# Two attention blocks on one core: query and key projections by seven half products in place of eight, with the combinations formed on chip

## The chip, the cores and the metric

The kernel runs on one core of a Trainium2 chip. The metric is the device time of one execution in microseconds (us), the median of several runs.

## What is computed

Two layers, one after the other, on x of shape (4, 32, 32, 768): four images of 1024 tokens with 768 channels. Each layer is a group normalisation, an attention with 12 heads of 64 channels and a positional bias, an output projection and a residual. All is float32. Cut to what matters (layer 1 differs by biases on queries, keys and values, and by the scale):

```python
xn = gn(x)                                   # 32 groups of channels
qkv = xn @ Wqkv                              # 768 -> 3 * 768
q, k, v = split(qkv)                         # per head: 1024 x 64
rel_h = einsum('bhwc,hkc->bhwk', q, Rh)      # bias by row distance
rel_w = einsum('bhwc,wkc->bhwk', q, Rw)      # bias by column distance
scores = scale * q @ k.T + rel_h[..., :, None] + rel_w[..., None, :]
out = softmax(scores) @ v
x = x + out @ Wproj + bproj
```

## The kernel before

**Tiling.** Channels lie on the 128 partitions, six chunks of them (NC = 6), tokens along the free dimension. Eight images are worked on in turn (two layers of four), each in six pairs of heads: 48 pairs, numbered g. A pair has eight units n, one for each 128 query tokens.

**A unit** (the loop over `units`, L566) works on three units at once: `biases` (L312) adds the two bias parts into tiles sc of unit n+2 on POOL; `scores` (L326) multiplies queries by keys for unit n+1 into PSUM (two buffers of 128x1024, one a head), VectorE adds the bias and takes the extreme of each row (L342), and ACT takes the exponential with its row sum (L346); `turn` (L358) transposes the finished sc of unit n in blocks on VectorE into tb, and every second unit writes tb to DRAM (td, L373); `divide` (L351) takes the reciprocal of the sums of unit n+1 on VectorE (L353) and multiplies on POOL (L356). `read_back` (L378) fetches td in another order as pt, a quarter of the queries at a time, and `weigh` (L386) multiplies pt by the values: quarters 0 and 1 of the pair at n=6, quarters 2 and 3 at n=2 of the next pair.

**What fills TensorE between.** While pair g is worked on, `prepare(g + 1)` supplies the projections of the next pair. `project_in` (L202) has four groups (queries or keys, left or right half of the tokens), each of six chunk steps; a step is two products of 64 contracted rows, the upper and the lower half of the partitions, which go to two PSUM areas t[0] and t[1] (the two halves of the array work side by side). ACT copies t[0] to SBUF and VectorE adds t[1] (L227 to L230). `project_values` (L237) does the same for two pairs at once in four groups, two of them in each pair. `put_out` gives groups of the output projection. `take` (L524) hands these out step by step, in the numbers of `shares`: [6, 6, 0, 6, 12, 6, 0, 12] steps in units 0 to 7, 48 a pair.

**Order.** The order of instructions on each engine is the order in which this program writes them; no scheduler moves them. Almost all DMAs are issued by SP, in that order, and a DMA that waits holds up those behind it. Work appended to `later` is issued two units on, work appended to `early` one unit on. `positions` (L269) multiplies the queries by the table of distances and writes the result to DRAM; `diagonals` (L295) reads it back with sixteen DMAs as rel. They follow the query groups: positions two units after each, the diagonals at n=4. Read-backs of quarters 1 and 3 are issued in the unit after their td; those of 0 and 2 two units after.

**Input.** The normalised image lies in six tiles xn of 128x1024, from nine buffers (AHEAD = 3); `load_x` (L88) fills them, `stats` (L147) takes the means and variances of chunks, `norm` (L156) forms those of the groups, and `apply` (L192) normalises on VectorE, for the next image in pair 4. Weights: two buffers of one kind for queries and keys, one for values.

## Time and profile before

| | before |
|---|---|
| median of 3 runs, us | 3506.68 (3505.36 to 3508.88) |
| profiled execution, us | 3508.77 |
| its span, us | 3507.0 |
| granted TensorE clock | 0.998 |
| DMA moved | 1084.54 MB, 309 GB/s in the mean |

The span is the time from the first to the last instruction of the profiled execution; 1.8 us of that execution lie around it. The page gives for each engine its busy time and share, then the costliest groups of instructions: line, engine, operation, output<-input, shape, count, then busy time, mean nanoseconds of one, idle time in front, and what ended that idle time. Matmuls on the two halves of the array overlap, so the mean of one (591 ns for pj) is longer than what each adds to the time; the distance between the starts of two groups tells that. A float32 matmul of the program is two records in the profile.

### The profile page before, as it was taken

The numbers are of one execution on the slowest core, as the hardware profiler recorded it, in microseconds if no ns is written. First come the engines' busy times: TensorE is split into PE (matmuls) and PEld (weight loads), VectorE is DVE, ScalarE is ACT, GpSimd is POOL, SyncE is SP. The second block draws the span as 40 slices with busy tenths as digits, with TensorE's granted clock in tenths as the row PEclk, the third lists the DMA queues.
The fourth block names the chain that finished last, engine by engine and source line by source line (L and its number), as shares of the span: only waits on it lengthen the run. The fifth ranks groups of instructions, "written<-read, shape, count | busy, mean of one in ns | idle before, by whom it ended". The sixth has DMA issues, their size and how long they took to land.

```text
span 3507.0 us, 55102 instructions
## 1 busy us (share of the span) xinstructions
PE 3462.3 (99%) x21120; PEld 1921.4 (55%) x21120; DVE 2381.1 (68%) x3676; ACT 1227.5 (35%) x2040; POOL 2729.9 (78%) x1546
## 2 busy tenths in 40 slices
PE   6999999999999999999999999999999999999999
PEld 4555555555555555555555555555555555555554
DVE  4666767767677676767767667666666667666666
ACT  2334333333333333333333333333333333333331
POOL 3888887778777787788777788787787778787774
PEclk9999999999999999999999999999999999999999
DMA  4889989999899898898989989899889988898877
GB/s 137 312 308 311 332 293 337 319 316 326 304 329 323 313 316 313 312 324 305 326 305 326 320 292 332 311 331 306 300 327 324 321 298 316 319 322 295 311 275 281
DMA packets 624857, 1084.54 MB, mean 309 GB/s; under 512 B 247120, under 2 KB 310096, under 8 KB 575440
## 3 DMA queue, kind: packets, MB, share of 16 engines
q1 hardware_dynamic: 569008, 1028.29, 83.4%
q10 hardware_dynamic: 55584, 52.72, 4.4%
q8 instruction: 166, 2.72, 0.3%
q14 instruction: 99, 0.81, 0.1%
HBM read 580.59 MB, written 500.27 MB: 308 GB/s over the span
## 4 chain that ended last, share of the span: by engine, by line
PE 97%; DMA 2%; DVE 0%; SPq 0%; issue 0%; ACT 0%; POOL 0%; ACTq 0%; DVEq 0%
PE pj L214 28%; PE s L333 19%; PE av L399 19%; PE o L475 14%; PE pv L249 14%; PE tp L281 3%; DMA tdr<-t 1%; DMA pt<-td 1%; SPq L307 0%; DMA td<-tb 0%; DMA wo<-in_wo 0%; DMA xn<-in_x 0%; DVE st L152 0%; DMA rel<-tdr 0%; DMA per<-mv 0%
## 5 line engine op out<-in xcount | busy, mean ns | idle before, releaser
L319 POOL TENSOR_TENSOR sc<-rel 128x1024 f32<-128x1024 f32 x768 | 1890.4, 2485 | 38.2 <-DMA rel<-tdr 38.2
L356 POOL TENSOR_SCALAR sc<-sc,sm 128x1024 f32<-128x1024 f32 x768 | 855.1, 1127 | 686.1 <-DVE sm L353 669.2
L346 ACT ACTIVATE sc<-sc,sm 128x1024 f32<-128x1024 f32 x768 | 879.8, 1147 | 1370.9 <-DVE sm L342 1368.7
L342 DVE CUSTOM_DVE_ANT_0 sc<-s,sc 128x1024 f32<-128x1024 f32 x768 | 909.8, 1222 | 293.3 <-PE s L333 266.4
L214 PE MATMUL pj<-xn,w 64*128 64x512 f32 x4608 | 1033.5, 591 | 26.8 <-DVE xn L193 25.7
L370 DVE STREAM_TRANSPOSE tb<-sc 128x1024 f32<-128x1024 f32 x768 | 910.7, 1222 | 22.9 <-DMA td<-tb 20.5
L214 PEld LDWEIGHTS pj<-xn,w 64*128 64x128 f32 x4608 | 453.2, 188 | 568.6 <-issue 536.6
L333 PE MATMUL s<-k,q 64*128 64x512 f32 x3072 | 750.1, 598 | 7.0 <-DVE sm L342 6.9
L399 PE MATMUL av<-pt,v 128*64 128x256 f32 x6144 | 689.1, 382 | 6.1 <-DMA pt<-td 6.1
L399 PEld LDWEIGHTS av<-pt,v 128*64 128x64 f32 x6144 | 434.5, 137 | 289.8 <-ACT v L259 35.6
L249 PE MATMUL pv<-wv,xn 64*128 64x256 f32 x4608 | 515.7, 376 | 0.0
L249 PEld LDWEIGHTS pv<-wv,xn 64*128 64x128 f32 x4608 | 448.3, 187 | 90.8 <-issue 30.1
L475 PE MATMUL o<-attn,wo 128*128 128x512 f32 x1080 | 475.8, 597 | 0.2 <-DMA wo<-in_wo 0.2
L333 PEld LDWEIGHTS s<-k,q 64*128 64x128 f32 x3072 | 288.5, 187 | 299.5 <-issue 275.5
L475 PEld LDWEIGHTS o<-attn,wo 128*128 128x128 f32 x1080 | 201.4, 190 | 271.4 <-issue 260.9
L260 DVE TENSOR_TENSOR v<-pv,v 128x256 f32<-128x256 f32 x192 | 81.5, 425 | 277.6 <-ACT v L259 277.6
L259 ACT COPY v<-pv 128x256 f32<-128x256 f32 x192 | 71.5, 372 | 330.7 <-PE pv L249 282.9
L286 ACT COPY t<-tp 128x1024 f32<-128x1024 f32 x96 | 97.2, 1012 | 245.5 <-PE tp L281 148.5
L346 ACT ACTIVATION_READ_ACCUMULATOR sc<-sc,sm 128x1 f32 x768 | 143.6, 187 | 0.0
L230 DVE TENSOR_TENSOR q<-pj,q 128x512 f32<-128x512 f32 x96 | 66.4, 692 | 107.5 <-ACT q L227 56.0
L230 DVE TENSOR_TENSOR k<-pj,k 128x512 f32<-128x512 f32 x96 | 66.4, 692 | 95.5 <-ACT k L227 49.0
L281 PEld LDWEIGHTS tp<-tab,q 64*128 64x128 f32 x1536 | 100.0, 187 | 39.9 <-issue 39.6
(34 smaller groups left out, 787.6 us busy)
## 6 DMA issues: line engine op xcount, KB each, us to landing
td<-tb SPq DMA_DIRECT2D x384, 1024.0 KB, 5.9
pt<-td SPq DMA_DIRECT2D x382, 1024.0 KB, 7.6
tdr<-t ACTq DMA_DIRECT2D x96, 512.0 KB, 6.3
w<-in_wqk SPq DMA_DIRECT2D x96, 384.0 KB, 7.5
rel<-tdr SPq DMA_DIRECT2D x760, 32.0 KB, 2.3
part<-res SPq DMA_DIRECT2D x84, 256.0 KB, 5.5
res<-part SPq DMA_DIRECT2D x84, 256.0 KB, 9.1
wv<-in_wv SPq DMA_DIRECT2D x24, 768.0 KB, 8.7
```

The costliest lines, as they stand in the source:

```text
L214: nc.tensor.matmul(t[:, a, :], lhsT=w[rows, c, :], rhs=xn[c][rows, cols], start=(c == 0), stop=(c == NC - 1),)
L230: nc.vector.tensor_tensor(to, t[1], to, ALU.add)
L249: nc.tensor.matmul(t[:, a, k, :], lhsT=xn[c][rows, (2 * i + k) * P : (2 * i + k + 1) * P], rhs=w[rows, c, :], start=(c == 0), stop=(c == N ...
L281: nc.tensor.matmul(ps[:, h, j, :], lhsT=q[rows, at * P : (at + 1) * P], rhs=tabs[l][rows, :], start=True, stop=True,)
L319: nc.gpsimd.tensor_tensor(sc.rearrange("p (a k) (u l) -> p a (k u) l", a=4, l=8), rel[:, h, 0, n, :].unsqueeze(1).unsqueeze(3).to_broadcas ...
L333: nc.tensor.matmul(ps[h][:, cols], lhsT=q[rows, n * P : (n + 1) * P], rhs=k[rows, cols], start=True, stop=True,)
L342: nc.vector.tensor_tensor_reduce(out=sc, in0=ps[h], in1=sc, scale=-scale, scalar=BIG, op0=ALU.add, op1=ALU.min, accum_out=st[:, 0, h : h + 1],
L346: nc.scalar.activation(sc, sc, AF.Exp, bias=st[:, 0, h : h + 1], scale=-1.0, accum_out=st[:, 1, h : h + 1],)
L356: nc.gpsimd.tensor_scalar(sc, sc, st[:, 2, h : h + 1], 1.0, ALU.mult, ALU.mult)
L370: nc.vector.transpose(tb[:, :, j, :], sc_of[g, n, h])
L399: nc.tensor.matmul(av[rows, at * 2 * P : (at + 1) * 2 * P], lhsT=v_of[g][:, k, rows], rhs=pt_of[g, quarter, h][:, :, k, :], start=(k == 0) ...
L475: nc.tensor.matmul(t, lhsT=wo_of[im, o, c], rhs=attn_of[im * NP + c][:, cols], start=(c == c0), stop=(c == c1 - 1),)
```

## The change

A product of two matrices cut into two by two blocks needs seven block products in Strassen's scheme instead of eight, at the price of sums of blocks. Here the blocks are the upper and lower half of the 128 partitions of a chunk (TOP and LOW) on the contracted side, queries and keys on the one outer side and the two halves of the tokens on the other. It is used for 39 of the 48 pairs; pair 0 of each image, and pair 1 of the first, stay `plain`.

- `project_in` has four units. Units 0, 2 and 3 have six chunk steps as before, each step two half products; unit 1 has three, since its one half product is spread over both halves of the partitions. `shares` gives 9 steps in n=0 and 6 in n=4 for these pairs (45 in all).
- `sum_weights` forms the weights' sums once for each of the 39 pairs, one pair ahead of the projection, at n=6 (ACT) and n=7 (VectorE and POOL). `sum_input` forms the input's sums once an image during pair 5 of the image before (for the first image during its pair 0), one chunk in each of n=0 to 5, and at n=6 and 7 subtracts the left from the right half in place.
- The right half's values are then restored in `project_values`: the products of the left half's upper rows are kept in v where the right half will come (`part`), and are added.
- x is in 21 tiles of 128x512, handed on from image to image by `make_room`. For the statistics of layer 0 all chunks pass through the tmp buffer; the loads for use come in pair 4. `apply` is on POOL for all images but the first.
- The transposed tile tb has two buffers instead of three. The weights w0, w1, w3 and w4 have one each. The table of layer 1 is loaded late into the place of that of layer 0. The last image's outputs lie in tiles of x.
- `biases` runs over the same elements in another order: the innermost loop has 32 elements with a step of 8 in the output.

```diff
-    tbpool = ctx.enter_context(tc.tile_pool(name="tb", bufs=3))
+    tbpool = ctx.enter_context(tc.tile_pool(name="tb", bufs=2))
...
+    def make_room(im):
+        x, y = x_of[im - 1], y_of[im - 1]
+        x_of[im] = y[NC:] + x[:NC] + y[:3]
+        y_of[im] = y[3:NC] + x[NC:]
...
-        def apply(c):
-            nc.vector.tensor_scalar(
-                xn_of[im][c], xn_of[im][c], nrm[:, c, 0:1], nrm[:, c, 1:2], ALU.subtract, ALU.mult
+        def apply(c, i):
+            x = x_of[im][i * NC + c]
+            (nc.gpsimd if im else nc.vector).tensor_scalar(
+                x, x, nrm[:, c, 0:1], nrm[:, c, 1:2], ALU.subtract, ALU.mult
             )
...
+            w, x = (
+                (w_of[g, 0], xs[:NC]), (w_of[g, 4], ys[NC:]),
+                (w_of[g, 3], xs[NC:]), (w_of[g, 1], ys[:NC]),
+            )[unit]
...
+        elif unit == 0:
+            nc.scalar.copy(k[0], t[0])
+            add(q[0], t[1], k[0], bias[0])
+        elif unit == 1:
+            add(k[0], t[0], k[0])
+            add(k[0], t[1], k[0])
+        elif unit == 2:
+            add(k[1], t[0], k[0])
+            add(q[1], t[1], k[1], bias[0])
         else:
+            add(k[1], t[0], k[1], bias[1])
+            add(k[0], t[0], k[0], bias[1])
+            nc.vector.tensor_tensor(k[0], k[0], t[1], ALU.subtract)
...
+        if g + 1 < NPAIR:
+            if unit == (1 if plain(g) else 0):
+                later.append(lambda: load_w(g + 1, 0))
+            if unit == 3:
+                early.append(lambda: load_w(g + 1, 1))
...
+        def first():
+            nc.scalar.copy(w3[TOP], w[1][LOW])
+
+        def second():
+            nc.vector.tensor_tensor(w3[TOP], w3[TOP], w[1][TOP], ALU.add)
+            nc.gpsimd.tensor_tensor(w3[LOW], w3[TOP], w[0][TOP], ALU.subtract)
+            nc.vector.tensor_tensor(w4[TOP], w3[TOP, :3], w[0][TOP, :3], ALU.subtract)
+            nc.vector.tensor_tensor(w4[LOW], w3[TOP, 3:], w[0][TOP, 3:], ALU.subtract)
+            nc.gpsimd.tensor_tensor(w3[LOW], w[0][LOW], w3[LOW], ALU.subtract)
+            nc.gpsimd.tensor_tensor(w[1][TOP], w[0][TOP], w[1][TOP], ALU.subtract)
...
+    def sum_input(im, n):
+
+        xs, ys = x_of[im], y_of[im]
+        if n < NC:
+            a, b, y, z = xs[n], xs[NC + n], ys[n], ys[NC + n % 3]
+            nc.scalar.copy(y[LOW], b[TOP])
+            nc.vector.tensor_tensor(y[TOP], b[LOW], y[LOW], ALU.subtract)
+            if n < 3:
+                nc.vector.tensor_tensor(z[TOP], y[TOP], a[TOP], ALU.add)
+                nc.vector.tensor_tensor(y[LOW], y[TOP], a[TOP], ALU.add)
+                nc.vector.tensor_tensor(y[LOW], y[LOW], a[LOW], ALU.subtract)
+            else:
+                nc.vector.tensor_tensor(z[LOW], y[TOP], a[TOP], ALU.add)
+                nc.vector.tensor_tensor(y[LOW], z[LOW], a[LOW], ALU.subtract)
+            return
+        for c in range(3 * (n - NC), 3 * (n - NC) + 3):
+            a, b = xs[c], xs[NC + c]
+            (nc.gpsimd if c < 3 else nc.vector).tensor_tensor(b[TOP], b[TOP], a[TOP], ALU.subtract)
...
-            nc.scalar.copy(to, t[:, 0, :, cols])
-            nc.vector.tensor_tensor(to, t[:, 1, :, cols], to, ALU.add)
+            part = v_of[g + h][:, 2 * i + 4 : 2 * i + 6, :] if i < 2 and g else to
+            if i < 2 or g == 0:
+                nc.scalar.copy(part, t[:, 0, :, cols])
+            else:
+                nc.vector.tensor_tensor(to, t[:, 0, :, cols], to, ALU.add)
+            nc.vector.tensor_tensor(to, t[:, 1, :, cols], part, ALU.add)
...
-            shape = [P, 4, HW, 8]
+            shape = [P, 4, 8, HW]
             nc.gpsimd.tensor_tensor(
-                sc.rearrange("p (a k) (u l) -> p a (k u) l", a=4, l=8),
-                rel[:, h, 0, n, :].unsqueeze(1).unsqueeze(3).to_broadcast(shape),
-                rel[:, h, 1, n, :].rearrange("p (l a) -> p a l", a=4).unsqueeze(2).to_broadcast(shape),
+                sc.rearrange("p (a k) (u l) -> p a l (k u)", a=4, l=8),
+                rel[:, h, 0, n, :].unsqueeze(1).unsqueeze(2).to_broadcast(shape),
+                rel[:, h, 1, n, :].rearrange("p (l a) -> p a l", a=4).unsqueeze(3).to_broadcast(shape),
...
-                shares = [6, 6, 0, 6, 12, 6, 0, 12]
+                shares = [6, 6, 0, 6, 12, 6, 0, 12] if g + 1 >= NPAIR or plain(g + 1) else [9, 6, 0, 6, 6, 6, 0, 12]
...
+            if pair == 4 and not end:
+                if n == 0:
+                    make_room(im + 1)
+                for c in range(3 * n - 3, 3 * n) if 1 <= n <= 4 else ():
+                    load_x(im + 1, c % NC, c // NC)
...
-            if pair == 4 and n == 7 and not end:
-                for chunks in ((3, 4), (5,)):
-                    take(todo, 3)
-                    share -= 3
-                    for c in chunks:
-                        apply(c)
+            if pair == 4 and n in (6, 7) and not end:
+                for c in range(4) if n == 6 else range(4, NX):
+                    apply(c % NC, c // NC)
+            if g + 2 < NPAIR and not plain(g + 2) and n in (6, 7):
+                if n == 6:
+                    sums = sum_weights(g + 2)
+                sums[n - 6]()
+            if pair == NP - 1 and not end:
+                sum_input(im + 1, n)
+            elif g == 0:
+                sum_input(0, n)
```

## The prediction

> **What bounds the kernel now.** I read the page from the top: busy time by engine, the slices, the chain of waits; then the cost groups, the list of waits, and stretches of the timeline around one pair of heads.
>
> ```profile
> PE 3462.3 (99%) x21120; PEld 1921.4 (55%) x21120; DVE 2381.1 (68%) x3676; ACT 1227.5 (35%) x2040; POOL 2729.9 (78%) x1546
> ...
> PE 97%; DMA 2%; DVE 0%; SPq 0%; issue 0%; ACT 0%; POOL 0%; ACTq 0%; DVEq 0%
> PE pj L214 28%; PE s L333 19%; PE av L399 19%; PE o L475 14%; PE pv L249 14%; PE tp L281 3%; DMA tdr<-t 1%; DMA pt<-td 1%; SPq L307 0%; DMA td<-tb 0%; DMA wo<-in_wo 0%; DMA xn<-in_x 0%; DVE st L152 0%; DMA rel<-tdr 0%; DMA per<-mv 0%
> ...
> L319 POOL TENSOR_TENSOR sc<-rel 128x1024 f32<-128x1024 f32 x768 | 1890.4, 2485 | 38.2 <-DMA rel<-tdr 38.2
> L356 POOL TENSOR_SCALAR sc<-sc,sm 128x1024 f32<-128x1024 f32 x768 | 855.1, 1127 | 686.1 <-DVE sm L353 669.2
> ```
>
> TensorE is 97% of the chain, and pj, the group that the change cuts, is its largest part. POOL has 686 us of idle in front of the divides; that is the whole margin it has. VectorE is at 68%. So TensorE work taken away is time taken away, unless something that now hides beneath it comes out. Where that could be, the timeline shows (start, length, engine, line, shape, count):
>
> ```profile
> 1722.03 1.89 PE L333 MATMUL s<-k,q 64*128 64x512 f32 x8
> 1723.75 5.32 PE L214 MATMUL pj<-xn,w 64*128 64x512 f32 x24
> 1728.90 1.88 PE L333 MATMUL s<-k,q 64*128 64x512 f32 x8
> 1730.61 5.32 PE L214 MATMUL pj<-xn,w 64*128 64x512 f32 x24
> 1735.76 5.35 PE L249 MATMUL pv<-wv,xn 64*128 64x256 f32 x48
> 1740.94 1.88 PE L333 MATMUL s<-k,q 64*128 64x512 f32 x8
> ```
>
> ```profile
> 1727.62 1.46 SPq L373 DMA_DIRECT2D td<-tb  x2
> 1729.17 10.31 SPq L307 DMA_DIRECT2D rel<-tdr  x16
> 1739.59 0.94 SPq L381 DMA_DIRECT2D pt<-td  x2
> ```
>
> The first shows one unit n=3 (6.87 us) and one n=4 (12.04 us, two groups in it). The second shows SP's queue in the same time: the sixteen rel transfers take 10.3 us to issue, and the read-back of quarter 1 comes behind them.
>
> **What the skill says, and whether the trace agrees.** (1) The Trainium skill, "SBUF — State Buffer", section "Who interferes with whom": a VectorE instruction in a two-port mode, or with two SBUF inputs, contends with a GpSimd instruction that reads SBUF; whoever comes second is blocked for a whole instruction. The normalisation shows this for the two-port kind:
>
> ```profile
> L193 DVE TENSOR_SCALAR xn<-xn,nrm x48: 808/1204/2620, 24.9 to 2987.3; 128x1024 f32<-128x1024 f32 x48
> ```
> (min/median/max ns). Alone it takes 808 ns. Its mean is 1470 (69.6 us for 48); leaving out the first six, the mean is (69.6 − 6×0.81)/42 = 1.54, so the other engine costs 0.7 us each time. No VectorE operation of the kernel before has two SBUF inputs, so for these no row exists. (2) "GPSIMD Engine Reference", section "Performance pitfalls for Q7 kernels": a read with a step above 8 bytes costs about 2.9 cycles an element instead of 1.9; section "Performance versus the Vector engine": an add of 2048 elements takes 4497 ns. The bias add now reads one input with a step of 16 bytes; its 2.485 us for 1024 elements are 2.9 cycles at the page's 1.2 GHz, which agrees.
>
> **The change part by part**, against the profiled run of 3508.8 us (span 3507.0; the median of the runs is 3506.7, 2 us less).
>
> *Products removed.* 39 of 48 pairs aren't plain. In each, three of 24 chunk steps go, that is 12 matmul records of 512 columns (each step has four: two row halves, two passes). A group of 24 records and the start of the next are 1728.90 − 1723.75 = 5.15 us apart, 0.2146 each. 39 × 12 × 0.2146 = 100.4 us, all on the chain.
>
> *Combining products.* A plain pair drains four products by four ACT and four VectorE instructions (0.69 us each); the others by one and eight. Four more VectorE adds are 2.8 us a pair. Values 2 and 3 move their first copy to VectorE: 4 × 0.42 = 1.7 us in every second pair. One input of each is PSUM, so the contention above does not apply. Beneath TensorE: a unit of VectorE is 4.7 us from its first score reduction to the reciprocal, and units last 6.9 to 12.4.
>
> *Weights.* 39 times on VectorE three adds at n=7 (64x768, twice 64x384: about 0.9 + 0.5 + 0.5 us at the element rate of the 512-column row), plus blocking; on POOL three of 64x768, about 1.7 us each by the page's 4497/2048 ns an element, 5.1 us a pair. n=7 lasts 12.4 us, while POOL needs 7.1 for biases and divides: 12.2, just covered. The normalisation moves to POOL too, 84 of about 0.6 us, mostly in n=7 of pair 4.
>
> *Sums of the input.* Once an image, in pair 5 (for the first image in its pair 0), VectorE gets four 64x512 adds in n=0 to 2, three in n=3 to 5 and in n=7. They have two SBUF inputs, follow one another, and start just as POOL starts divides and biases. I take 0.62 us each and 0.6 us of blocking (from 0.0 to 1.1: the latter if each of them lets one POOL instruction pass). A unit is then 4.7 + 4×1.22 + 0.7 = 10.3 us for n=0 to 2, 9.1 for n=3, 9.9 for n=4, 9.2 for n=5, 5.4 for n=6 and 15.1 for n=7 (sums, weights, four outputs of 0.75); TensorE's units in these lines are 7.0, 7.8, 9.9, 6.9, 12.0, 6.9, 8.9, 12.4. VectorE falls behind by 3.3, 2.5, 0.4, 2.2, gains 2.1, loses 2.3, gains 3.5, loses 2.7. It may lag by about the unit less 3.4 us before the next scores find no free PSUM. Stepping through that, TensorE stands 2.7 us at n=3, 0.4 later, 1.1 at the next pair's start: 4.2 us an image, 34 us for eight. With 0 us of blocking nothing stands; with 1.1 us it is 9.6 an image, 77.
>
> *Read-back of quarter 1.* In the pairs with seven products n=4 takes 6 steps instead of 12: the weighing of n=6 comes 5.1 us earlier. The read-back doesn't: SP issues sixteen rel transfers first (10.3 us), and now also the second weight, which was behind it. Before, it was issued at 1739.6 and 1740.1, lands 7.6 us later (the page's median), 1747.7, and was needed half-way through the weighing at 1749.65 + 3.56 = 1753.2. Now it is needed at 1748.1 and lands at about 1748.2. Nothing is left over; with a scatter of one or two us I take 0.6 us a pair, 39 × 0.6 = 23 us (0 to 1.5 a pair).
>
> *Two buffers for the transposed tile instead of three.* The even units' transposes must wait for the write of the unit before. At 3 to 4 and 5 to 6 the gap is some 5.6 us, the median landing 5.9: VectorE waits about a microsecond, sometimes more, three times a pair. Beneath TensorE, as VectorE has about 58 of 70 us to do; uncovered it would be some 2 us a pair.
>
> *Bias add with the other loop order.* Reads become contiguous, writes get a step of 32 bytes. By the page's add, 2.25 us (estimate); nothing shows strided writes on POOL. Bounds 2.0 to 3.5. It is off the chain up to a point given below. The table of layer 1 loaded late, x in halves, 4.7 MB more of loads for statistics, other buffers for the last outputs: 0 (±3), as TensorE waits for none of them in the list of waits.
>
> Sum: 3508.8 − 100.4 + 34 + 23 = 3465; on the median's basis 3463.
>
> **Rivals.** *Everything stays hidden.* For it: engines other than TensorE have slack over any whole pair; two applications at n=2 and n=4 took 0.86 us, nearly unblocked. Against: they met POOL at a lucky moment. 3506.7 − 100.4 = 3406, to 3416. *The sums meet POOL one for one.* For it: the three applications of n=7 took 5.0 us instead of 2.4. 3463 + (77 − 34) = 3506, no change. *POOL becomes the bound (slower).* Place: the bias add, 768 times. Price: 77 us per 0.1 us. The rest of POOL is 855 + 199 (weights) + 50 (normalisation) + 26 (sums of n=6) = 1130 us, so POOL fills the 3406 us from 2.96 us an add and exceeds the old time from 3.1; at 3.3 it gives 3665. For it: if writes cost by their step as the page says of reads, 32 bytes is past its 8. Against: the old order had a read of that kind, which goes.
>
> **How the numbers follow.** Forecast 0.42, own range 3435 to 3495; all hidden 0.22; one for one 0.17 (it spills to both sides of no change); POOL bound 0.16; others 0.03. Under 0.2%, 7 us, a measurement of this kernel can't tell from no change. Faster: 0.42 + 0.22 + 0.06 + 0.01 = 0.71; same 0.06; slower 0.16 + 0.06 + 0.01 = 0.23. The range reaches from all hidden to just beyond one for one: 3405 to 3520, leaving out the bound by POOL.
>
> **What would show it.** 468 fewer pj records, of the same 0.21 us. In the list of waits, scores waiting for VectorE in each pair 5 and at n=3 above all, about 4 us an image; av waiting for pt by some 0.6 us a pair; the input's adds at about 1.2 us in the mean, with a minimum near 0.6; the bias add below 2.485 us. Wrong I am if the bias add is above 2.9, or if TensorE stands in ordinary pairs for something else: late weights, a drained product, the transposed tile's write.

## The result, and the profile after

| | before | after |
|---|---|---|
| median of 4 runs, us | 3507.62 (3505.36 to 3508.88) | 4081.73 (4075.33 to 4093.54) |
| ratio, 95% interval | | 1.1641 (1.1612 to 1.1671) |
| profiled execution, us | 3508.77 | 4075.33 |
| its span, us | 3507.0 | 4073.3 |
| granted TensorE clock | 0.998 | 0.947 |

The changed kernel is 16% slower, where the prediction had 3463 us and a range up to 3520. First the page of after: busy time by engine, the granted clock by slice, the chain of waits by engine and by line.

```profile
PE 3568.1 (88%) x20652; PEld 1936.1 (48%) x20652; DVE 2951.5 (72%) x4197; ACT 1177.7 (29%) x1918; POOL 2893.8 (71%) x1771
...
PEclk9999899998999989999899998999989999899999
...
PE 51%; DVE 19%; DMA 16%; POOL 7%; issue 4%; SPq 2%; ACT 0%; DVEq 0%; ACTq 0%
PE pj L262 17%; DMA td<-tb 12%; PE av L514 11%; PE s L448 10%; PE o L590 6%; PE pv L364 5%; DVE tb L485 5%; POOL x L223 4%; DVE sc L457 3%; DMA pt<-td 2%; PE tp L396 2%; SPq L422 2%; DVE x L334 2%; POOL sc L434 1%; DVE x L345 1%
```

TensorE has 468 records less than before (21120 to 20652), as the scheme promises, but the chain that ends last no longer runs through it: its share fell from 97% to 51%, and the write of the transposed tile (td<-tb) alone has 12%. Two amounts make up the 566 us. TensorE idles 505 us instead of 45 (span less busy time): 460 more. And it is busy 106 us longer in spite of 100 us less work: 3568.1 against 3462.3 − 100.4 = 3361.9, 206 us more. Most of that is the lower clock: the trace's clock records put TensorE at half clock for 434 us (17 before), it was busy in 292 of them, and half of those, some 146 us, would have been saved at full clock. The other 60 us are not explained. The list of waits says who is late (total, times, longest, in us); before, the first of these lines was 20.5 in all, 6.5 at most, and the second 6.1 in all:

```profile
DVE tb L485 <- DMA td<-tb: 378.0, 121, 9.6
PE av L514 <- DMA pt<-td: 110.6, 49, 4.1
PE o L590 <- DVE res L599: 103.0, 15, 15.5
PEld pj L262 <- POOL x L223: 88.7, 52, 3.4
PE o L590 <- DVE res L601: 84.0, 25, 4.6
```

So VectorE waits for the write (td, before its transposes), TensorE for the read-back (pt) and for VectorE to drain the output groups (res) from PSUM.

**An ordinary pair.** The lengths of the units, worked out from the starts of the first score reduction of each unit, are means over images 1 to 6, in us. n=4 has six steps less (5.15 us) and n=0 three more (2.57), so that a pair should take 69.1 in place of 71.7:

```
                n=0    n=1    n=2    n=3    n=4    n=5    n=6    n=7
before, any     6.88   7.75   9.88   6.94  11.97   7.02   8.85  12.41
after, pair 1   9.76   7.44   9.87   7.05   6.78   6.82  14.27  17.32
after, pair 5  22.00  16.75  12.65   9.11  10.30   9.70   5.74  26.13
```

n=0 to n=5 of pair 1 are about as long as their steps (n=4 is 5.2 us shorter, n=0 2.9 longer), and n=6 and n=7 give back 10. Why shows in the timeline of after, SP's queue first (start, length, engine, line, count):

```profile
2131.93 1.46 SPq L488 DMA_DIRECT2D td<-tb  x2
2133.48 10.35 SPq L422 DMA_DIRECT2D rel<-tdr  x16
2143.94 0.38 SPq L126 DMA_DIRECT2D w<-in_wqk  x1
2144.37 0.98 SPq L496 DMA_DIRECT2D pt<-td  x2
2145.70 1.46 SPq L488 DMA_DIRECT2D td<-tb  x2
```

The write of n=5 is issued at 2145.7, directly behind the 2 MB of the read-back at 2144.4 and the weight. Before, n=4 lasted five microseconds longer and the two stood apart. The chain of waits of after has the landing, VectorE's and TensorE's timelines what follows (in brackets the idle time in front):

```profile
2146.82 12.97 DMA td<-tb
```

```profile
2157.60 1.25 DVE L485 STREAM_TRANSPOSE tb<-sc 128x1024 f32<-128x1024 f32 x1 [6.19 <-DMA td<-tb]
```

```profile
2167.81 0.93 DVE L319 TENSOR_TENSOR w<-w,w 64x768 f32<-64x768 f32 x1
2168.77 1.35 DVE L321 TENSOR_TENSOR w<-w,w 64x384 f32<-64x384 f32 x1
2170.14 1.38 DVE L322 TENSOR_TENSOR w<-w,w 64x384 f32<-64x384 f32 x1
2171.54 0.69 DVE L601 TENSOR_TENSOR res<-o,res 128x512 f32<-128x512 f32 x1
```

```profile
2159.52 8.22 PE L590 MATMUL o<-attn,wo 128*128 128x512 f32 x18
...
2172.29 5.30 PE L590 MATMUL o<-attn,wo 128*128 128x512 f32 x6 [4.55 <-DVE res L601]
```

The write needs 13 us where the page's median is 6.0. With two buffers the transposes of n=6 stand for it 6.19 us, and VectorE is behind from there on. In n=7 the three sums of the weights (3.7 us together) come directly ahead of the drain of an output group (L601), so both delay that drain. TensorE runs out of PSUM, stands 4.55 us, and does the next six records in 5.30 us where eighteen had taken 8.22 (2.74 for six). The Trainium skill, "TensorE: Matmul & The Clock Gate", part 1, says that after an idle window of about 3.4 us the array runs at half its clock until a window of that length has been busy. The granted clock is 0.50 from 2172.29 to 2177.28, which agrees; but shorter stops were enough too. By the clock records of after, half clock began during, or within 3.4 us after, all 32 of TensorE's idle stretches longer than 4 us, 34 of the 47 between 2 and 4 us, and 2 of the 41 between 1 and 2 us.

That the transfers have no room just there shows in stretches of the trace (length, busy times, granted clock, share of the DMA engines, GB/s). After, then before, first the rel transfers, then what comes behind them:

```profile
2132.00:2144.00 12.00, 12.00 (x94) 8.67 (x92) 11.27 (x19) 3.01 (x6) 9.52 (x7) 1.00 0.70 215
2144.00:2159.00 15.00, 13.91 (x109) 8.65 (x106) 8.07 (x14) 5.00 (x9) 9.09 (x6) 1.00 0.95 336
```

```profile
1727.60:1739.60 12.00, 12.00 (x76) 7.14 (x74) 7.25 (x11) 3.87 (x8) 10.74 (x7) 1.00 0.70 215
1739.60:1750.00 10.40, 10.40 (x82) 7.47 (x82) 6.56 (x12) 3.88 (x8) 5.53 (x5) 1.00 0.89 318
```

While the sixteen small transfers are issued, 215 GB/s move; behind them the engines are 95% busy for 15 us at 336 GB/s. Read-back and write share that, and both are late: TensorE waits for pt in n=6 in many of the pairs (the 110.6 us above), VectorE for the write.

**Pair 5 and the end of pair 4.** POOL now normalises, eight tiles in one block in n=7 of pair 4; the next pair's first sum on VectorE follows. POOL's and VectorE's timelines of after:

```profile
1992.15 17.00 POOL L223 TENSOR_SCALAR x<-x,nrm 128x512 f32<-128x512 f32 x8
...
2015.16 3.96 POOL L434 TENSOR_TENSOR sc<-rel 128x1024 f32<-128x1024 f32 x2
2019.03 2.21 POOL L471 TENSOR_SCALAR sc<-sc,sm 128x1024 f32<-128x1024 f32 x2
2021.20 3.95 POOL L434 TENSOR_TENSOR sc<-rel 128x1024 f32<-128x1024 f32 x2
```

```profile
2016.72 8.91 DVE L334 TENSOR_TENSOR x<-x,x 64x512 f32<-64x512 f32 x1
```

A normalisation takes 2.1 us, not the 0.6 of the prediction, and the 17 us push biases and divides behind it. The sum, 64x512, ends only after POOL's row of instructions: 8.91 us, where a sum of this size takes 0.69 us in the mean in another place (L338 of e6, below). The costliest groups on the page hold the two POOL operations that the prediction priced (busy, mean ns of one):

```profile
L434 POOL TENSOR_TENSOR sc<-rel 128x1024 f32<-128x1024 f32 x768 | 1563.5, 2105 | 37.5 <-DMA rel<-tdr 37.5
...
L223 POOL TENSOR_SCALAR x<-x,nrm 128x512 f32<-128x512 f32 x84 | 176.6, 2115 | 0.0
```

**Where the time is lost.** For each pair, its length in after less what it had before (less 2.57 us, the twelve records, where the next pair has seven products), summed by place, in us. e4 to e16 are experiments below:

```
                        after   e4   e5   e9   e15  e16
pair 5          (7)      285   296  167  141  103  106
pair 4          (7)       67    42   56   -2   32   33
pair 0, image 0 (1)       22    22   22   20   20   20
pairs 0 to 3 of images 0 to 2, without it (11)
                         117    76  119   78   75   39
all others     (21)      179    50  179   44   16   15
sum                      670   486  544  281  245  213
```

670 − 100 is the difference of the spans to 4 us (pair ends differ a little from span ends).

### The profile page after: what moved, and what is told of

The parts are those of the page before. It is cut to its first block, busy times and chain, and to the rows that moved or that the text cites. A ratio compares the mean times of both kernels' runs of the same rounds, so it can differ in the third digit from the quotient of the medians.

```text
span 4073.3 us, 55032 instructions
## 1 busy us (share of the span) xinstructions
PE 3568.1 (88%) x20652; PEld 1936.1 (48%) x20652; DVE 2951.5 (72%) x4197; ACT 1177.7 (29%) x1918; POOL 2893.8 (71%) x1771
## 4 chain that ended last, share of the span: by engine, by line
PE 51%; DVE 19%; DMA 16%; POOL 7%; issue 4%; SPq 2%; ACT 0%; DVEq 0%; ACTq 0%
PE pj L262 17%; DMA td<-tb 12%; PE av L514 11%; PE s L448 10%; PE o L590 6%; PE pv L364 5%; DVE tb L485 5%; POOL x L223 4%; DVE sc L457 3%; DMA pt<-td 2%; PE tp L396 2%; SPq L422 2%; DVE x L334 2%; POOL sc L434 1%; DVE x L345 1%
## 5 line engine op out<-in xcount | busy, mean ns | idle before, releaser
L471 POOL TENSOR_SCALAR sc<-sc,sm 128x1024 f32<-128x1024 f32 x768 | 916.2, 1204 | 1083.3 <-DVE sm L468 1076.5
L434 POOL TENSOR_TENSOR sc<-rel 128x1024 f32<-128x1024 f32 x768 | 1563.5, 2105 | 37.5 <-DMA rel<-tdr 37.5
L485 DVE STREAM_TRANSPOSE tb<-sc 128x1024 f32<-128x1024 f32 x768 | 917.8, 1225 | 381.3 <-DMA td<-tb 378.0
L262 PE MATMUL pj<-x,w 64*128 64x512 f32 x4140 | 950.8, 601 | 81.0 <-POOL x L223 44.3
L514 PE MATMUL av<-pt,v 128*64 128x256 f32 x6144 | 763.7, 401 | 195.8 <-DMA pt<-td 110.6
L590 PE MATMUL o<-attn,wo 128*128 128x512 f32 x1080 | 555.2, 668 | 189.4 <-DVE res L599 103.0
L262 PEld LDWEIGHTS pj<-x,w 64*128 64x128 f32 x4140 | 410.4, 190 | 589.6 <-issue 450.6
L364 PE MATMUL pv<-wv,x 64*128 64x256 f32 x4608 | 515.1, 376 | 0.4 <-DVE k L238 0.4
L364 PEld LDWEIGHTS pv<-wv,x 64*128 64x128 f32 x4608 | 448.0, 187 | 91.6 <-issue 40.9
L223 POOL TENSOR_SCALAR x<-x,nrm 128x512 f32<-128x512 f32 x84 | 176.6, 2115 | 0.0
L599 DVE SCALAR_TENSOR_TENSOR res<-o,bo,res 128x512 f32<-128x512 f32 x88 | 64.4, 745 | 91.0 <-PE o L590 90.7
L601 DVE TENSOR_TENSOR res<-o,res 128x512 f32<-128x512 f32 x92 | 62.0, 683 | 70.1 <-PE o L590 69.4
```

Source lines behind the costliest of these rows:

```text
L223: (nc.gpsimd if im else nc.vector).tensor_scalar(x, x, nrm[:, c, 0:1], nrm[:, c, 1:2], ALU.subtract, ALU.mult)
L262: nc.tensor.matmul(t[:, a, :], lhsT=w[rows, c, :], rhs=x[c][rows, :], start=(c == 0), stop=(c == len(x) - 1),)
L364: nc.tensor.matmul(t[:, a, k, :], lhsT=xs[i // 2 * NC + c][rows, at * P : (at + 1) * P], rhs=w[rows, c, :], start=(c == 0), stop=(c == NC ...
L434: nc.gpsimd.tensor_tensor(sc.rearrange("p (a k) (u l) -> p a l (k u)", a=4, l=8), rel[:, h, 0, n, :].unsqueeze(1).unsqueeze(2).to_broadcas ...
L471: nc.gpsimd.tensor_scalar(sc, sc, st[:, 2, h : h + 1], 1.0, ALU.mult, ALU.mult)
L485: nc.vector.transpose(tb[:, :, j, :], sc_of[g, n, h])
```

## The experiments

Each was executed once beside the kernel before, except e14; a single time has no interval, and differences below some 20 us are not read (the four runs of after lie 18 us apart). Kernel before in these series: 3506.2 to 3509.7 (medians).

**e1, e2, e3: the kernel before with one or both of two features of the change.** No Strassen product is in them.

```diff
-    tbpool = ctx.enter_context(tc.tile_pool(name="tb", bufs=3))
+    tbpool = ctx.enter_context(tc.tile_pool(name="tb", bufs=2))
```

> The kernel before with two tb buffers instead of three, nothing else. Theory Q (the write of the transposed tile is late because it stands behind a read-back in the DMA queue, which happens only where the unit n=4 is short): the units keep their lengths, VectorE waits 1 to 3 us a pair, hidden, and the time stays at 3507 to 3520. Theory B (two buffers alone cost it): about 8 us a pair more, 3800 or above.

```diff
-                shares = [6, 6, 0, 6, 12, 6, 0, 12]
+                shares = [12, 6, 0, 6, 6, 6, 0, 12]
```

> The kernel before with twelve steps in n=0 and six in n=4 (the total stays 48), three tb buffers. Theory Q: the read-back of quarter 1 and the write of n=5 now stand one behind the other, but a third buffer is free for one head; some wait for the other head and for pt in the weighing: 3510 to 3600. Theory B: 3507 to 3515, since the number of buffers alone decides.

> Both edits on the kernel before: short n=4 and two tb buffers. Theory Q: the wait of the changed kernel appears here without any Strassen work, 5 to 7 us at n=6 and a few more at n=7, in all pairs: 3507 + 47 x 8 = about 3880. Theory B: the same as two buffers alone. Theory S (the wait comes from VectorE's added sums): 3507 to 3550.

Measured: e1 3510.36, e2 3938.93, e3 (both edits) 4041.43. Two buffers alone cost nothing that can be told from noise (4 us), though VectorE waits for the write 168.6 us in all instead of 20.5: the cover that the prediction named holds. The group of transposes of e1 (busy, mean ns, then idle time in front):

```profile
L370 DVE STREAM_TRANSPOSE tb<-sc 128x1024 f32<-128x1024 f32 x768 | 922.6, 1228 | 177.3 <-DMA td<-tb 168.6
```

e2 costs 433 us with all eight products and three buffers, but it is not the test of a short n=4 that it was meant to be. With twelve steps in n=0 both halves of the queries are finished one unit earlier, so `positions` and the rel transfers move one unit up as well, the transfers from n=4 to n=3. The lengths of its units, as in the table above:

```
                n=0    n=1    n=2    n=3    n=4    n=5    n=6    n=7
e2, pair 1     12.02   9.48   9.27   6.67  15.10   6.00   9.70  12.35
```

A pair is 8.9 us longer, and 8.3 of these stand in n=4, which with its six steps should take 6.8. n=6 and n=7, where the changed kernel loses its time, are nearly as in the kernel before. SP's and VectorE's timelines of e2 (the first line has the last two of the sixteen rel transfers):

```profile
1699.87 0.95 SPq L307 DMA_DIRECT2D rel<-tdr  x2
1700.91 0.95 SPq L381 DMA_DIRECT2D pt<-td  x2
1701.95 1.24 SPq L373 DMA_DIRECT2D td<-tb  x2
```

```profile
1712.71 1.25 DVE L370 STREAM_TRANSPOSE tb<-sc 128x1024 f32<-128x1024 f32 x1 [10.33 <-DMA td<-tb]
```

Again rel, read-back and write stand one behind the other and the transposes are late; but here they are the read-back of quarter 0, the write of n=3 and the transposes of n=4. So e2 shows that such a row of transfers costs 8 or 9 us a pair without any of Strassen's sums when it begins in n=3, which lasts 6.9 us, and not in n=4, which lasts 12 in the kernel before. What the short n=4 costs in the changed kernel it does not show; that is for e4 and e15. e3 is 103 us above e2, in the same place (n=4 17.69): where the write is late, a missing third buffer costs more. No run gives the changed kernel a third buffer.

**e4: the changed kernel with n=4 at its old length**, n=7 short instead.

```diff
-                shares = [6, 6, 0, 6, 12, 6, 0, 12] if g + 1 >= NPAIR or plain(g + 1) else [9, 6, 0, 6, 6, 6, 0, 12]
+                shares = [6, 6, 0, 6, 12, 6, 0, 12] if g + 1 >= NPAIR or plain(g + 1) else [9, 6, 0, 6, 12, 6, 0, 6]
```

> The changed kernel with twelve steps in n=4 and six in n=7 for its 39 pairs. Theory Q: the write of n=5 no longer stands behind the read-back, unit n=6 goes from 13.6 to about 8.9 us, and of the 9 us too much in each of these pairs 5 to 9 go, less what now stands at n=0 since n=7 is short: 3750 to 3900. Theory B or S: within 1% of 4080.

Measured 3892.18, clock 0.955. n=6 of pair 1 falls from 14.27 to 9.13, n=7 from 17.32 to 10.97. Ordinary pairs ("all others") lose 50 us instead of 179, pair 5 as much as ever. TensorE's waits for pt fall from 110.6 to 10.8 us, VectorE's for the write from 378.0 to 239.8. All of Strassen's products and sums are still there, so in ordinary pairs most of the loss belongs to the place from which the steps are taken. With six steps less n=7 should take 12.41 − 5.15 = 7.3: part of the wait has moved there.

**e5: the normalisation back on VectorE**, three tiles in each of n=3 to 6 of pair 4, ahead of the transposes.

```diff
-            (nc.gpsimd if im else nc.vector).tensor_scalar(
+            nc.vector.tensor_scalar(
...
+            if pair == 4 and 3 <= n <= 6 and not end:
+                for c in range(3 * n - 9, 3 * n - 6):
+                    apply(c % NC, c // NC)
             share = shares[n]
...
-            if pair == 4 and n in (6, 7) and not end:
-                for c in range(4) if n == 6 else range(4, NX):
-                    apply(c % NC, c // NC)
```

> The changed kernel with the next image's normalisation on VectorE for every image, three half tiles in each of n=3 to 6 of pair 4, ahead of the transposes; nothing else. Theory N (the normalisation on POOL, 2.1 us each, holds up biases and TensorE in pair 5): n=0 and n=1 of pair 5 go from 22.0 and 16.8 to about 11 us, pair 5 from 112 to about 95, the time to 4075 - 7 x 17 = 3955. Theory K (all of pair 5 is the contention of the input's sums): within 1% of 4080, since the sums keep their place.

Measured 3950.66: 131 us less; pair 5 falls from 112.4 to 95.5 us (n=0 from 22.0 to 11.5, n=1 from 16.8 to 11.5). The block on POOL cost 17 us an image.

**e6: e5 with the input's sums ahead of the transposes**, before POOL starts its divides.

```diff
+            if pair == NP - 1 and not end:
+                sum_input(im + 1, n)
+            elif g == 0:
+                sum_input(0, n)
             turn(g, n)
...
-            if pair == NP - 1 and not end:
-                sum_input(im + 1, n)
-            elif g == 0:
-                sum_input(0, n)
             take(todo, share)
```

> As the run before it, and the input's sums are issued between the score reductions and the transposes instead of behind the reciprocal. Theory K (in their old place they start together with POOL's divides and biases): POOL has mostly run dry there, the sums take 0.7 to 0.8 us each instead of 1.5, and pair 5 goes to 75 to 82 us: 4075 - 7 x 33 = about 3845. Theory V (VectorE has too many instructions, wherever they stand): pair 5 stays within 4 us of the run before.

Measured 3950.68, pair 5 95.9 us: no gain. Groups of e5, then of e6:

```profile
L338 DVE TENSOR_TENSOR x<-x,x 64x512 f32<-64x512 f32 x24 | 56.2, 2341 | 0.8
```

```profile
L334 DVE TENSOR_TENSOR x<-x,x 64x512 f32<-64x512 f32 x48 | 69.6, 1450 | 94.3 <-ACT x L333 94.3
...
L338 DVE TENSOR_TENSOR x<-x,x 64x512 f32<-64x512 f32 x24 | 16.5, 689 | 0.8
```

The contention of this sum was there and is gone (2.34 to 0.69 us), but the first sum of each unit now waits 2 us for ACT's copy, which stands behind the exponentials, and the transposes wait with it. One wait took the other's place.

**e7: e6 with the shares of e4.**

> As the run before it, with twelve steps in n=4 and six in n=7. If the three causes (write behind read-back, normalisation on POOL, place of the sums) are separate, their savings add up: 3892 - 7 x 33 = about 3660, with regular pairs at 70 to 72 us. If they cover each other, it stays above 3750.

Measured 3748.36, clock 0.969; pair 5 still 99.5. TensorE's and VectorE's timelines of e7 in n=7 of a pair 5:

```profile
1935.23 5.49 PE L590 MATMUL o<-attn,wo 128*128 128x512 f32 x6 [9.77 <-DVE res L599]
```

```profile
1922.48 5.95 DVE L345 TENSOR_TENSOR x<-x,x 64x512 f32<-64x512 f32 x3
```

Three of the last sums take 5.95 us; two transposes and the weights' sums (3.7 us) follow, and the drain of an output group stands behind all of them: TensorE waits 9.77 us for it.

**e8: e7 without the input's sums** of images 1 to 7.

```diff
-            if pair == NP - 1 and not end:
-                sum_input(im + 1, n)
-            elif g == 0:
+            if g == 0:
```

> The run with all three edits (normalisation on VectorE, sums ahead of the transposes, long n=4), without the input's sums for images 1 to 7: the projections of those images take old contents of these tiles, the work on TensorE is the same. If the sums are what is left in pair 5, it goes from 99 to 72 us and the time from 3748 to 3748 - 7 x 27 = 3560, with less half-clock time on TensorE. If what is left there is something else (loads, the weights' sums, the transposed tile), pair 5 stays above 85.

Measured 3613.09: 135 us less, pair 5 from 99.5 to 80.9. That is what the sums cost in that arrangement; the prediction had 34. Pair 5 is not at 72: n=0 takes 13.6 behind the short n=7, and n=7 15.95 with the weights' sums.

**e9: e7 with the sums in another order**: ACT's copy a unit earlier, all six subtractions in place at n=6 (which has no other work), the weights' sums of n=7 behind its output groups.

```diff
-            nc.scalar.copy(y[LOW], b[TOP])
...
+            elif pair == NP - 1 and not end:
+                copy_low(im + 1, n + 1)
...
             turn(g, n)
...
-                sums[n - 6]()
+                    sums[0]()
             take(todo, share)
+            if g + 2 < NPAIR and not plain(g + 2) and n == 7:
+                sums[1]()
```

> The same three edits with the sums kept, but in another order: ACT's copy for a chunk one unit earlier, VectorE's three subtractions in place at n=6 instead of n=7 (all six there), and the weights' sums of n=7 behind the drains of PSUM instead of ahead of them. If TensorE stands in pair 5 and at n=7 because drains queue behind sums on VectorE, pair 5 goes to 78 to 84 us, n=7 of pair 5 from 23.6 to about 13, and the time to 3550 to 3620. If the amount of work counts and not its order: above 3700.

Measured 3686.62: 62 us less with every sum in place. n=7 of pair 5 falls from 23.6 to 13.5, the pair to 91.7; I had expected 78 to 84. n=0 to 2 (13.6, 11.0, 12.5) did not move, so the early copy brought less than thought: what remains there is put down to VectorE's own time, which no run isolates. Ordinary pairs gain little: "all others" lose 44 us, 52 in e7.

**e10: the changed kernel with half of the rel transfers on ACT's queue.**

```diff
-                    (nc.scalar if h and not g else nc.sync).dma_start(
+                    (nc.scalar if h else nc.sync).dma_start(
```

> The changed kernel with the eight rel transfers of the second head issued by ACT instead of SP; nothing else. Theory Q in its form 'SP's sixteen issues hold the read-back of quarter 1 back until it stands just ahead of the write of n=5': the read-back is issued 5 us earlier, the write of n=5 lands in 6 to 9 us instead of 13, n=6 goes from 13.6 to 9 to 11, and the time to 3850 to 3980, less what ACT's delayed exponentials cost. If SP's issues don't matter: within 1% of 4080, or above.

Measured 4141.35, slower by 60. ACT's and SP's timelines of e10:

```profile
2250.30 6.71 ACTq L422 DMA_DIRECT2D rel<-tdr  x8
```

```profile
2256.95 3.77 SPq L422 DMA_DIRECT2D rel<-tdr  x8
...
2262.50 0.98 SPq L496 DMA_DIRECT2D pt<-td  x2
```

The two halves came one after the other, 10.5 us together as on one queue, and the read-back is no earlier. By SP's list of waits its half stood for a rel transfer that ACT had issued (SP waits for rel 216.7 us in 77 times; 0.9 us in after): SP's first was issued only as those of ACT landed. The Trainium skill, "DMA: Bandwidth & Descriptors", section "Issuing engines are not separate DMA queues", says that a second issuing engine saves only issue time; as the program made one half wait for the other, no run here shows it. ACT's exponentials now stood behind its eight. Nor does the run tell what an earlier read-back would do.

**e11: the read-back of quarter 1 behind the write of n=5**, not ahead of it.

```diff
-                (behind if quarter % 2 else behind2).append(
+                (held if quarter == 1 else behind if quarter % 2 else behind2).append(
...
             turn(g, n)
+            if n == 5:
+                run(held)
```

> The changed kernel with one edit: the read-back of quarter 1 is issued behind the transposes and the write of n=5, not at the start of n=4 ahead of it. Shares stay as changed (n=4 short). Theory (the write of n=5 lands late only because it stands behind the read-back in SP's queue): it lands some 6 us after issue instead of 13, VectorE's wait of 6.2 us before the transposes of n=6 goes, n=6 falls from 14.3 to 9 or 10 us and n=7 from 17.3 to about 12.5, a regular pair from 78.5 to 69 or 71; times 39, 3720 to 3790 us in all, from 4082. The wait of av for pt in n=6 may grow by a microsecond or two. Rival A (the short n=4 leaves too little time between the two writes, wherever the read-back stands): the write of n=5 still lands at about the same time, n=6 stays at 13 or more, total 4030 to 4120. Rival B (the two only change places): the write lands early but the read-back of quarter 1 now lands late, TensorE waits for pt in n=6 by some 5 us, n=6 stays at 13 or more and n=7 falls only in part; 3900 to 4080.

Measured 4293.34, slower by 212: rival B, and worse than it said. VectorE's wait for the write falls from 378.0 to 134.7 us, but now the read-back is later still: TensorE's own waits for it, all in n=6 (19.7 us long), go from 110.6 to 355.9 us. SP's and TensorE's timelines of e11 (the four read-backs are two of quarter 1 and, behind them, two of quarter 2):

```profile
2496.22 1.46 SPq L488 DMA_DIRECT2D td<-tb  x2
2497.74 6.56 SPq L496 DMA_DIRECT2D pt<-td  x4
```

```profile
2496.67 3.67 PE L514 MATMUL av<-pt,v 128*64 128x256 f32 x32
2506.63 1.12 PE L514 MATMUL av<-pt,v 128*64 128x256 f32 x2 [6.29 <-DMA pt<-td]
2509.34 6.23 PE L514 MATMUL av<-pt,v 128*64 128x256 f32 x30 [1.59 <-DMA pt<-td]
```

The queue position decides which of the two is later, not whether one is. With e4 this says that what counts is the time from the rel transfers to n=6, in which 4 MB must pass.

**e12: e9 with the late read-back and the changed kernel's shares.**

> All edits that helped so far in one kernel: normalisation on VectorE in n=3 to 6 of pair 4, sums of the input ahead of the transposes and in the order of e9, the late read-back of e11, and the changed kernel's own shares (n=4 short, n=7 long). Theory: regular pairs 69 to 71 us, pair 5 about 84 (e9's 91.5 less the long n=0 that followed a short n=7), pair 0 of the first image 85: 3507 - 100 + 7 x 15 + 20 + 39 x 1 = 3530 to 3590 us, slower than before by one or two per cent. If the late read-back did not help (rival A or B of e11), 3800 or more. If the sums and weights weigh more with a long n=7, pair 5 stays at 91 or more and the total is 3590 to 3640.

Measured 4060.67: ordinary pairs are at 78 to 82 us, n=6 at 19.3, as e11's theory had failed. Beside e11 the run shows one thing more. Of the edits that it adds, only the order of the weights' sums in n=7 touches ordinary pairs, and these fall from 84.0 to 79.9 us (pair 1). TensorE's waits for the drains of output groups, 165.9 us in e11 and 187.0 in after, are no longer in the list. So with a short n=4 the weights' sums ahead of the drains cost some 4 us a pair; with a long one (e9 against e7) 0.4.

**e13, e14: the steps taken from n=1**, in the changed kernel and in e9.

```diff
-                shares = [6, 6, 0, 6, 12, 6, 0, 12] if g + 1 >= NPAIR or plain(g + 1) else [9, 6, 0, 6, 6, 6, 0, 12]
+                shares = [6, 6, 0, 6, 12, 6, 0, 12] if g + 1 >= NPAIR or plain(g + 1) else [6, 3, 0, 6, 12, 6, 0, 12]
```

> The changed kernel with one edit: the steps of a pair with seven products are spread 6, 3, 0, 6, 12, 6, 0, 12 in place of 9, 6, 0, 6, 6, 6, 0, 12, so that n=4 and n=7 keep the lengths that they have in the kernel before and n=1 is the short unit, 2.6 us shorter. Theory (the loss in regular pairs comes from the two units whose length covers the write, rel and read-back, n=4 and n=7, and not from the products or their sums as such): n=4 about 12, n=6 about 9, n=7 about 12.4, n=0 about 7; a regular pair at 69 to 71.5 us (n=1 may wait a microsecond or two at its end for the transposed tile), so 39 x 8 = 310 us below the changed kernel, pair 5 somewhat shorter too (its n=0 waits as before, its n=7 26): 3690 to 3790 us. Rival A (two buffers for the transposed tile, or the sums of the weights in n=7, cost most of it wherever the work is taken): regular pairs at 75 or more, 3880 or more.

> The same spread of steps together with the edits of e5, e6 and e9 (normalisation on VectorE in n=3 to 6 of pair 4, sums of the input ahead of the transposes, in the order of e9). Theory: regular pairs 69 to 71.5, pair 5 about 82 to 86 (91.5 in e9, less the long n=0 behind a short n=7), pair 0 of the first image about 85: 39 x 70 + 7 x 84 + 85 + the rest gives 3480 to 3560 us, about the time of the kernel before; under 3500 would show that half of the products' gain can be kept. Rival: the sums of the weights and of the input in a long n=7 of pair 5 cost TensorE as much as in e7; pair 5 at 91 or more, 3570 to 3640 us. If regular pairs stay at 75 or more (rival A of the run beside it), 3700 or more.

Measured: e13 4194.42; e14 3871.15 (3865.22 to 3877.98 in 4 runs), ratio 1.1044 (1.1025 to 1.1062). These runs answer another question than they were made for. With this spread the second half of the queries is finished at n=3, not n=1, so `positions` and rel come two units later, at n=6, when POOL needs rel at once. The list of waits of e13:

```profile
POOL sc L434 <- DMA rel<-tdr: 396.0, 77, 39.7
```

n=6 is back at 9.4 as expected, and n=7 takes 21.6 instead. (In these two the positional terms of half the queries of one pair, before the change of layers, come from the other layer's table, which is loaded in between.) What remains of use: 15 of the 45 steps must be done by n=1, so the steps can only be taken at n=3 or later. e2 had moved them the other way. And in e14 pair 5 is 86.8, its n=0 8.3 instead of 13.6: the long n=0 of e7 to e9 belonged to the short n=7.

**e15: e9 with the loss shared between n=4 and n=7.**

```diff
-                shares = [6, 6, 0, 6, 12, 6, 0, 12] if g + 1 >= NPAIR or plain(g + 1) else [9, 6, 0, 6, 12, 6, 0, 6]
+                shares = [6, 6, 0, 6, 12, 6, 0, 12] if g + 1 >= NPAIR or plain(g + 1) else [9, 6, 0, 6, 9, 6, 0, 9]
```

> The kernel of e9 with the steps spread 9, 6, 0, 6, 9, 6, 0, 9: n=4 and n=7 each give up three steps where e9 took six from n=7 alone. The rel transfers stay where they are (unlike in e13 and e14, where the late second half of the queries moved them to n=6). Theory (the lateness is a burst of transfers that has to fit between the transposes of n=3 and of n=6, and likewise behind n=7; each microsecond taken from one of these covers beyond its slack costs one): n=4 9.2, n=6 about 11.5, n=7 about 13, n=0 8; pair 5 about 88 (n=0 about 11, n=7 15), regular pairs 70 to 73: total 3610 to 3700 us, beside e9's 3687 and above the kernel before in any case. Rival (the short n=4 alone matters and it has a threshold): with 9 steps n=6 and n=7 are as before, regular pairs at 69, total under 3560.

Measured 3648.59, within the theory's 3610 to 3700; clock 0.982. Units of pair 1: n=4 9.31, n=6 11.25, n=7 12.10, n=0 8.03. With six, nine and twelve steps in n=4 (after, e15, e4), n=6 takes 14.27, 11.25 and 9.13 us. This is the best version with all of its work, 140 us above the kernel before. From its page:

```profile
PE 3437.0 (94%) x20652; PEld 1915.3 (53%) x20652; DVE 2956.2 (81%) x4281; ACT 1170.3 (32%) x1918; POOL 2661.1 (73%) x1687
```

TensorE is busy 3437 − 3362 = 75 us longer than its work should take, not 206. In the 21 pairs of "all others" 0.8 us above the expected 69.1 are left (16 us): there most of the products' gain is kept, and a pair lasts 69.9 us in the mean instead of 71.7.

**e16: e15 without the second loads of the input** for the statistics of images 1 to 3.

```diff
-                passing = tmppool.tile([P, S], FP, tag="tmp", name=f"x_{im + 1}_{c}")
                 for i in range(2):
-                    x = passing[:, i * HALF : (i + 1) * HALF]
-                    load_x(im + 1, c, i, x)
+                    x = x_of[im][i * NC + c]
```

> The kernel of e15 with one part left out: the inputs of images 1 to 3 are no longer loaded a second time to pass through the tmp buffer for their statistics; the same statistics instructions read the resident tiles of the image being worked on instead (so these statistics are those of other data). Theory (the passing loads, 512 KB at n=5 and at n=7 of three pairs in images 0 to 2, fall into the stretches in which the transfers have no slack, and share the tmp buffer with the positions): the eleven pairs 0 to 3 of images 0 to 2, which stand 75 us above their share in e15, come down to 10 to 25 us above, total 3585 to 3600 us. Rival (these pairs are long for another reason, such as the output's own transfers or layer 0's drains): they stay at 60 us or more above, total 3635 to 3655.

Measured 3616.97: 32 us less. Pairs 0 to 3 of images 0 to 2 stand 39 us above their share instead of 75, between theory and rival. The loads cost about half of it; the other half is open.

## Why the prediction was wrong

By its own steps:

- **Products removed, −100.4: right.** 468 records went, and e15's undisturbed pairs show the 2.6 us a pair less 0.8.
- **Read-back of quarter 1, +23: the step that failed.** It saw the place, the rel transfers and the lost cover of n=4, but priced the lateness of the read-back alone, at 0.6 us a pair, as if the transfers behind it had room. TensorE waits for pt 110.6 us, 2.8 us for each of the 39 pairs. And the next transfer in the queue, the write of n=5, which the shorter unit moved up against the read-back, is late too: it takes 13 us, and VectorE waits 378.0 us for writes where it had waited 20.5. Giving n=4 its length back (e4) brings 190 us.
- **Two buffers for the transposed tile, 0: right alone (e1), wrong in the sum.** It took the median landing of 5.9 us from the page. That median belongs to the old distances; here the write takes 13. Where the write is late the third buffer is missed: e3 is 103 us above e2. In the changed kernel itself no run isolates it.
- **Sums of the input, +34 (0 to 77): right in kind, mis-sized.** They cost 135 us (e8 against e7). The term priced the blocking by POOL; e6 took the blocking away and gained nothing. Much of the cost is that PSUM drains stand behind the sums in VectorE's order (e7): e9 gets 62 us back by order alone, that of the weights' sums included.
- **Weights, covered: not so in n=7.** The cover was worked out for POOL; on VectorE the three adds take 1.26, 1.51 and 1.38 us in the mean of after (0.9, 0.5 and 0.5 in the prediction) and stand ahead of the drains of n=7. e12 against e11 puts some 4 us a pair on that order where n=4 is short. In the changed kernel itself no run isolates it.
- **The normalisation on POOL, "84 of about 0.6 us": mis-sized.** 2.115 us each; e5 shows 131 us. No row of before had this operation on POOL, and the prediction kept no bounds for it.
- **Bias add, 2.25 (2.0 to 3.5): right.** 2.105 us; the slower rival, POOL as the bound by this operation, fell. The change did become slower, but not by that mechanism.
- **The loads for statistics, 0 (±3): wrong.** Some 32 us in the arrangement of e15 (e16), in stretches where the transfers have no slack.
- **Missing altogether: the clock.** TensorE's waits of more than about 2 us mostly lowered its clock, and some 146 of the 566 us are its own work done slower. Every estimate of a stall was priced at the stall's length alone.

The range went wrong with it: each term was bounded as if the others stayed as they were, while the queue's spacing, which all of them lean on, was what the change moved.

That no version here beats the kernel before is shown only for those tried. In e15 103 us are left in pair 5; removing them and the 75 of the early images would give about 3470, an estimate from the table, and no run has shown it.

## What to carry to other kernels

When work is removed from the bounding engine, look at what its length separated: list the DMAs issued in the shortened unit and the next, and ask whether they still fit between, in bytes over the rate that the stretch shows; a median landing time from the old trace holds only for the old spacing. Take removed work from the units that cover no burst, and see whether the moved steps move a burst with them, earlier (e2) or later (e13). Put additions behind the drains that the bounding engine waits for, not before (e9, e12). In after TensorE's stalls of more than 2 us mostly, and those of more than 4 us always, came with half clock: count such a stall at more than its length.

## What the runs showed of the hardware that was not expected

- In after, a subtract-and-multiply with two per-partition scalars on POOL takes 2115 ns for 512 elements a partition in the mean; the multiplication by one such scalar takes 1204 ns for 1024.
- The Trainium skill, "SBUF — State Buffer", section "Who interferes with whom", has the second comer blocked for a whole instruction. Here a VectorE add with two SBUF inputs lasted 8.91 us, through the rest of one POOL instruction and the five that followed without a gap; the lock was not handed over between them. The means of the input's adds in after are 1.05 to 2.2 us.
- POOL's bias add fell from 2485 to 2105 ns when its reads became contiguous and its writes got a step of 32 bytes. VectorE's adds into the queries, with a step of 16 bytes in what they write, take 1110 ns (1172 with a bias) where those into the keys take 689 (747).
- What an idle stretch costs TensorE beyond itself: 64 records of av took 2.6 us more behind one of 12.15 us. TensorE's timeline of after, in a pair 5:

```profile
2028.54 9.76 PE L514 MATMUL av<-pt,v 128*64 128x256 f32 x64 [12.15 <-DVE q L238]
...
2066.86 7.13 PE L514 MATMUL av<-pt,v 128*64 128x256 f32 x64
```
